# A first convolution in three bf16 products per tap instead of one f32 product

## The chip, the cores and the metric

The kernel runs on one NeuronCore of a Trainium2 chip. The metric is the device time of one execution in microseconds. The engines are named as in the profile: PE is the matrix engine (PEld its weight loads), DVE the vector engine, ACT the scalar engine, POOL GpSimd, and SP the engine from whose queue the transfers are issued. The core has an on-chip memory of 128 partitions (SBUF) and a smaller one into which PE accumulates (PSUM).

## The reference

Four layers follow one another on a tensor x of 64 images, 128 channels, 28x28 points, all f32. Only the first is touched:

```
out = conv3x3(x, quant_weight(w1))          # 128 -> 128 channels, 3x3, padding 1
out = batchnorm(out, gamma1, beta1)         # mean and variance over all images
out = quant_act(out)                        # clip to 0..1, 16 levels
out = conv3x3(out, quant_weight(w2 * m))
out = batchnorm(out, gamma2, beta2) + identity
out = quant_act(out)
```

The quantised weights are odd whole numbers from -15 to 15, divided by 15; the kernel keeps the whole numbers and moves the factor into the batch-norm. The next layers are a self-attention over the points of each image, a Mamba block that scans each image in four directions, and a second Mamba block over eight tokens in each point, with a group-norm and a residual.

## The kernel before, in words

The channels lie on the 128 partitions; an image is 784 columns (T), half an image 392 (HT). The function conv_block does the whole first layer. It begins with the helper quantised, once for each set of weights: a transfer, a Tanh on ACT, the maximum over the row (DVE) and over the partitions (POOL), and a few DVE instructions up to the whole numbers. The last of these, line 168, writes the tile q in the type that the caller names: f32 for the first convolution (line 171), bf16 for the second (line 172).

The first loop (line 175) takes two images at a time, 32 groups in all. A group is loaded into the tile xt (line 177, SP's queue). For each image, conv3x3 makes 18 matmuls: two halves of 14 rows, nine taps each, accumulated in one PSUM bank a half. A tap is a shifted window of the image, cut off at the border, so a matmul has 351 to 392 columns. ACT copies both halves from PSUM to the tile raw (line 182), DVE takes two statistics of it (line 184), and the group is stored to memory (line 185). The batch-norm (line 101 and what follows) needs the statistics of all images. The second loop (line 192) loads the groups again, scales and rounds them (ACT line 196, DVE lines 197 and 199) into the bf16 tile qa, convolves them with the same conv3x3, and copies out and stores image by image (lines 204 to 207). A second batch-norm closes the layer.

The tiles xt, raw, act and qa lie in a pool with three buffers for each name (line 144); the second loop's loads use the name xt too. The PSUM tile acc, one image in two banks, has four buffers. In conv_block the order of instructions on each engine is not written out by hand: the framework orders the traced instructions by the timeline of its own simulation (line 1495), earlier ones first where they can start, and places the waits. Each engine then works in that order.

The attention and the first Mamba block, by contrast, are ordered by a planner in the kernel (class Plan), with costs of its own, and issued in exactly that order (line 469). The token block after them is again left to the framework.

Of the kernel before, what the change touches and what calls it, by code (L numbers as in the profile page):

```python
# [16 lines left out]
F32 = mybir.dt.float32  # L17
BF16 = mybir.dt.bfloat16
AF = mybir.ActivationFunctionType
ALU = mybir.AluOpType  # L20
# [5 lines left out]
C = 128  # L26
HW = 28
T = HW * HW
# [34 lines left out]
def halves(ap):  # L63
    return ap.rearrange("p (h x) -> p h x", h=2)


@with_exitstack
def tile_kernel(ctx: ExitStack, tc: tile.TileContext, x, w1t, w2t, m2t, vecs, pk3, pk4, out):
    nc = tc.nc
    NB = x.shape[0]  # L70

    cpool = ctx.enter_context(tc.tile_pool(name="cpool", bufs=1))
    dram = ctx.enter_context(tc.tile_pool(name="dram", bufs=1, space=DRAM))

    vec = cpool.tile([C, NVEC], F32, name="vec")
    nc.sync.dma_start(vec, vecs)

    def v(name, i=0, p=C):
        a = VEC_AT[name][0] + i
        return vec[:p, a : a + 1]  # L80

    ident = cpool.tile([C, C], F32, name="ident")
    make_identity(nc, ident)
    eps = cpool.tile([C, 1], F32, name="eps")
    nc.vector.memset(eps, BN_EPS)
    x2d = [dram.tile([C, T], F32, name=f"x2d{b}") for b in range(NB)]

    utd = [dram.tile([C, 2, T], F32, name=f"utd{b}") for b in range(NB)]
    ztd = [dram.tile([C, 2, T], F32, name=f"ztd{b}") for b in range(NB)]

    c2d, s2, b2x15 = conv_block(tc, cpool, dram, x, w1t, w2t, m2t, v, eps)
    tables = Tables(tc)
    tables.use(EXP_LN)
    attention_and_mamba(tc, tables, x, c2d, s2, b2x15, x2d, utd, ztd, pk3, pk4, vec, v, ident, eps)
    token_mamba(tc, tables, x2d, utd, ztd, pk4, v, ident, eps, out, NB)


def bn_affine(nc, pool, stats, gamma, beta, unit, eps, name):

    mv = pool.tile([C, 2], F32, name=f"mv{name}")  # L100
    nc.vector.bn_aggr(mv, stats.rearrange("p n s -> p (n s)"))
    std = pool.tile([C, 1], F32, name=f"std{name}")
    nc.scalar.activation(std, mv[:, 1:2], AF.Sqrt, bias=eps, scale=unit * unit)
    rstd = pool.tile([C, 1], F32, name=f"rstd{name}")
    nc.vector.reciprocal(rstd, std)
    s = pool.tile([C, 1], F32, name=f"s{name}")
    nc.vector.tensor_scalar(s, rstd, gamma, unit, ALU.mult, ALU.mult)
    ms = pool.tile([C, 1], F32, name=f"ms{name}")
    nc.vector.tensor_mul(ms, mv[:, 0:1], s)
    b15 = pool.tile([C, 1], F32, name=f"b15{name}")  # L110
    nc.vector.tensor_sub(b15, beta, ms)
    nc.vector.tensor_scalar(b15, b15, 15.0, None, ALU.mult)
    return s, b15


def conv3x3(nc, ps, w, src):

    img = src.rearrange("p (h w) -> p h w", w=HW)
    taps = [(0, 0)] + [(dy, dx) for dy in (-1, 0, 1) for dx in (-1, 0, 1) if (dy, dx) != (0, 0)]
    for half in range(2):  # L120
        acc = ps[:, half, :HT].rearrange("p (h w) -> p h w", w=HW)
        r0 = half * 14
        for i, (dy, dx) in enumerate(taps):
            lo, hi = max(r0, -dy), min(r0 + 14, HW - dy)
            a, b = max(0, -dx), min(HW, HW - dx)
            nc.tensor.matmul(  # L126
                acc[:, lo - r0 : hi - r0, a:b],
                lhsT=w[:, (dy + 1) * 3 + dx + 1, :],
                rhs=img[:, lo + dy : hi + dy, a + dx : b + dx],
                start=(i == 0),  # L130
                stop=(i == len(taps) - 1),
            )


def conv_block(tc, cpool, dram, x, w1t, w2t, m2t, v, eps):
    nc = tc.nc
    NB = x.shape[0]
    GRP = 2
    c1d = [dram.tile([C, GRP, T], F32, name=f"c1d{b}") for b in range(NB // GRP)]
    c2d = [dram.tile([C, T], F32, name=f"c2d{b}") for b in range(NB)]  # L140

    with ExitStack() as ctx:
        wp = ctx.enter_context(tc.tile_pool(name="wq", bufs=1))
        big = ctx.enter_context(tc.tile_pool(name="cv", bufs=3))
        ps = ctx.enter_context(tc.tile_pool(name="cvps", bufs=4, space=PSUM))

        def quantised(name, src, mask, dtype):

            w = wp.tile([C, 9 * C], F32, name="w", tag="wtmp", bufs=2)
            nc.sync.dma_start(w, src)  # L150
            if mask is not None:
                m = wp.tile([C, 9 * C], F32, name="m", tag="wtmp2")
                nc.sync.dma_start(m, mask)
                nc.vector.scalar_tensor_tensor(w, m, 0.5, w, ALU.is_gt, ALU.mult)
            t = wp.tile([C, 9 * C], F32, name="t", tag="wtmp3", bufs=2)
            nc.scalar.activation(t, w, AF.Tanh)
            mx = wp.tile([C, 1], F32, name=f"mx{name}")
            nc.vector.tensor_reduce(mx, t, AX.X, ALU.max, apply_absolute_value=True)
            mxa = wp.tile([C, 1], F32, name=f"mxa{name}")
            nc.gpsimd.partition_all_reduce(mxa, mx, C, bass_isa.ReduceOp.max)  # L160
            r = wp.tile([C, 1], F32, name=f"r{name}")
            nc.vector.tensor_scalar(r, mxa, 2.0, None, ALU.mult)
            nc.vector.reciprocal(r, r)
            nc.vector.tensor_scalar(t, t, r, 0.5, ALU.mult, ALU.add)
            nc.vector.tensor_scalar(t, t, 15.0, MAGIC, ALU.mult, ALU.add)
            nc.vector.tensor_scalar(t, t, MAGIC, 2.0, ALU.subtract, ALU.mult)
            q = wp.tile([C, 9, C], dtype, name=f"q{name}")
            nc.vector.tensor_scalar(q.rearrange("p k c -> p (k c)"), t, 15.0, None, ALU.subtract)  # L168
            return q

        q1 = quantised("1", w1t, None, F32)
        q2 = quantised("2", w2t, m2t, BF16)

        st1 = wp.tile([C, NB * 2, 6], F32, name="st1")
        for g in range(NB // GRP):
            xt = big.tile([C, GRP, T], F32, name="xt")
            nc.sync.dma_start(xt, x[g * GRP : (g + 1) * GRP].rearrange("b c t -> c b t"))
            raw = big.tile([C, GRP, T], F32, name="raw")
            for k in range(GRP):
                acc = ps.tile([C, 2, 512], F32, name="acc")  # L180
                conv3x3(nc, acc, q1, xt[:, k, :])
                nc.scalar.copy(halves(raw[:, k, :]), acc[:, :, :HT])
                for h in range(2):
                    nc.vector.bn_stats(st1[:, (g * GRP + k) * 2 + h, :], raw[:, k, h * HT : (h + 1) * HT])
            nc.sync.dma_start(c1d[g], raw)

        s1, b1x15 = bn_affine(nc, wp, st1, v("gamma1"), v("beta1"), 1.0 / 15.0, eps, "1")
        s1x15 = wp.tile([C, 1], F32, name="s1x15")
        nc.vector.tensor_scalar(s1x15, s1, 15.0, None, ALU.mult)

        st2 = wp.tile([C, NB * 2, 6], F32, name="st2")
        for g in range(NB // GRP):
            ld = big.tile([C, GRP, T], F32, name="xt")
            nc.sync.dma_start(ld, c1d[g])
            act = big.tile([C, GRP, T], F32, name="act")
            nc.scalar.activation(act, ld, AF.Relu, bias=b1x15, scale=s1x15)
            nc.vector.tensor_scalar(act, act, 15.0, MAGIC, ALU.min, ALU.add)
            qa = big.tile([C, GRP, T], BF16, name="qa")
            nc.vector.tensor_scalar(qa, act, MAGIC, None, ALU.subtract)
            for k in range(GRP):  # L200
                acc = ps.tile([C, 2, 512], F32, name="acc")
                conv3x3(nc, acc, q2, qa[:, k, :])
                raw = big.tile([C, T], F32, name="raw2")
                nc.scalar.copy(halves(raw), acc[:, :, :HT])
                for h in range(2):
                    nc.vector.bn_stats(st2[:, (g * GRP + k) * 2 + h, :], raw[:, h * HT : (h + 1) * HT])
                nc.sync.dma_start(c2d[g * GRP + k], raw)

        s2, b2x15 = bn_affine(nc, cpool, st2, v("gamma2"), v("beta2"), 1.0 / 225.0, eps, "2")
    return c2d, s2, b2x15  # L210
# [1288 lines left out]
```

## Time and profile before

| | us |
|---|---|
| median of 3 runs | 14449.58 (14403.58 to 14459.57) |
| profiled execution | 14456.75 |
| its span, first to last instruction | 14454.9 |
| first convolution on PE | 18.6 to 744.6 |
| second convolution on PE | 755.3 to 943.8 |
| PE busy over the span | 10855.2 (75%) |
| DVE busy over the span | 12706.4 (88%) |
| ACT busy over the span | 10460.3 (72%) |
| POOL busy over the span | 11391.7 (79%) |

The span is that of one execution taken by the profiler. The line number in a row (L126) is the line of the kernel that issued the instruction; L126 is the matmul in conv3x3 and serves both convolutions. In a row of the view by time, the first number is the start, the second the duration, both in us, then engine, line, operation, tiles (written <- read), shapes and type, and in brackets how long the engine was idle before and what released it. In a row of the groups, the numbers after the first bar are busy us and the mean ns of one record, those after the second the idle time before. A matmul's record is longer than its share of the stream, because the records of neighbours overlap.

### The profile page before, as it was taken

To read this page: it belongs to the slowest core of one execution; us is meant where nothing else is said; L and a number is where in the kernel's file an instruction comes from. 1 tells how busy PE (TensorE), PEld (TensorE's weight loads), DVE (VectorE), ACT (ScalarE), POOL (GpSimd) and SP (SyncE) were. 2 spreads that over 40 slices of the span, in tenths; PEclk is the share of its full clock that TensorE was granted. 3 is DMA by queue.
4 is the path that set the end of the run, shared out by engine and by line. 5 is a ranking of instruction groups with operands and counts; after the bars stand their busy time and mean duration, and the time that the engine had idled before them with its cause. 6 is when DMAs were issued, how large, how long until landed. Compare 5 with 4: busy or idle time off the path is not lost. (4 is left out here: it accounts for less than half of the span.)

```text
span 14454.9 us, 181149 instructions
## 1 busy us (share of the span) xinstructions
PE 10855.2 (75%) x58370; PEld 7180.2 (50%) x58370; DVE 12706.4 (88%) x13524; ACT 10460.3 (72%) x25236; POOL 11391.7 (79%) x5304
## 2 busy tenths in 40 slices
PE   9987777777777777777776676776767767677676
PEld 5654444444444444444443455555555555555554
DVE  1048999999999999999999799999999999999998
ACT  0047777777777777777777677777777777777776
POOL 0007899889898888889889788888888887888887
PEclk9988888888888888888887787888878888888787
DMA  2243444444444444444444211111112111111111
GB/s 74 72 162 109 135 123 128 129 121 127 131 121 126 130 120 124 133 122 124 134 121 125 67 45 46 55 48 52 45 48 60 44 49 47 49 59 42 49 50 44
DMA packets 711515, 1297.64 MB, mean 90 GB/s; under 512 B 206624, under 2 KB 357536, under 8 KB 710560
## 3 DMA queue, kind: packets, MB, share of 16 engines
q1 hardware_dynamic: 710560, 1286.05, 29.8%
q8 instruction: 460, 7.54, 0.2%
q14 instruction: 495, 4.06, 0.1%
HBM read 954.72 MB, written 330.76 MB: 89 GB/s over the span
## 5 line engine op out<-in xcount | busy, mean ns | idle before, releaser
L228 ACT ACTIVATE a<-delta,A 128x98 f32<-128x98 f32 x14336 | 3906.2, 365 | 1123.2 <-PE y L1317 827.4
L472 POOL TENSOR_TENSOR h<-ur,Br 128x784 f32<-128x784 f32 x1920 | 4205.3, 2216 | 152.6 <-PE y L472 136.3
L1293 POOL TENSOR_TENSOR db<-u,BC 128x896 f32<-128x896 f32 x1568 | 3274.0, 2101 | 856.0 <-DVE h L1312 688.1
L1317 PE MATMUL y<-a,ident 128*128 128x280 f32 x7168 | 2089.5, 455 | 954.2 <-DVE a L1310 898.5
L472 DVE TENSOR_TENSOR_SCAN ah<-ah,h 128x392 f32<-128x392 f32 x2304 | 2303.1, 1000 | 60.8 <-ACT ah L472 50.3
L1317 PEld LDWEIGHTS y<-a,ident 128*128 128x128 f32 x7168 | 1557.7, 221 | 1512.4 <-POOL db L1293 729.1
L472 DVE TENSOR_TENSOR_SCAN h<-a,h 128x784 f32<-128x784 f32 x768 | 1915.0, 2498 | 112.7 <-ACT a L472 57.9
L472 ACT ACTIVATE ah<-dr,A 128x392 f32<-128x392 f32 x2304 | 1322.9, 587 | 612.8 <-DVE ah L472 592.4
L472 POOL TENSOR_TENSOR h<-h,Cr 128x784 f32<-128x784 f32 x640 | 1350.7, 2114 | 357.9 <-DVE h L472 347.5
L1308 DVE TENSOR_TENSOR h<-h,a 128x896 f32<-128x896 f32 x1344 | 1473.7, 1096 | 33.1
L472 DVE TENSOR_TENSOR h<-ah,Cr 128x392 f32<-128x392 f32 x2304 | 1302.5, 565 | 72.9
L472 PE MATMUL y<-h,fold 128*32 128x98 f32 (+1 forms) x12288 | 1024.0, 422 | 385.2 <-DVE h L472 357.2
L1312 DVE TENSOR_TENSOR h<-h,db 128x896 f32<-128x896 f32 x1120 | 1228.2, 1097 | 59.1 <-POOL db L1293 0.5
L472 POOL TENSOR_TENSOR xn<-s,sq 128x784 f32<-128x784 f32 x64 | 136.5, 2133 | 1183.6 <-ACT sq L472 1142.9
L472 PEld LDWEIGHTS bank<-vt,et 112*112 112x112 f32 x6272 | 905.4, 215 | 233.9 <-ACT et L472 90.6
L1310 DVE TENSOR_TENSOR a<-h,BC 128x896 f32<-128x896 f32 x896 | 974.1, 1087 | 21.4
L472 PE MATMUL bank<-vt,et 112*112 112x128 f32 x6272 | 981.6, 320 | 5.0 <-ACT et L472 2.3
L1319 PE MATMUL y<-late,ident 128*128 128x112 f32 x7168 | 848.0, 275 | 14.3 <-DVE late L1310 13.4
L1319 PEld LDWEIGHTS y<-late,ident 128*128 128x128 f32 x7168 | 838.5, 193 | 37.8 <-DVE late L1310 18.0
L472 PEld LDWEIGHTS y<-h,fold 128*32 128x32 f32 x12288 | 378.8, 121 | 909.7 <-DVE h L472 428.8
L472 ACT ACTIVATE a<-dr,A 128x784 f32<-128x784 f32 x768 | 716.8, 942 | 152.0 <-DVE h L472 150.4
L126 PE MATMUL acc<-xt,q 128*128 128x378 f32 (+3 forms) x2304 | 726.0, 478 | 18.6 <-DVE q L168 18.6
(213 smaller groups left out, 20969.2 us busy)
## 6 DMA issues: line engine op xcount, KB each, us to landing
Br<-bcd SPq DMA_DIRECT2D x1536, 98.0 KB, 2.4
Cr<-bcd SPq DMA_DIRECT2D x1536, 98.0 KB, 2.4
dr<-dud SPq DMA_DIRECT2D x1280, 98.0 KB, 2.4
ur<-dud SPq DMA_DIRECT2D x1280, 98.0 KB, 2.3
utd<-tok SPq DMA_DIRECT2D x128, 392.0 KB, 2.7
ztd<-tok SPq DMA_DIRECT2D x128, 392.0 KB, 3.7
rows<-utd SPq DMA_DIRECT2D x192, 256.0 KB, 2.8
xt<-in_x SPq DMA_DIRECT2D x32, 784.0 KB, 5.2
```

The source lines that it names most:

```text
L126: nc.tensor.matmul(acc[:, lo - r0 : hi - r0, a:b], lhsT=w[:, (dy + 1) * 3 + dx + 1, :], rhs=img[:, lo + dy : hi + dy, a + dx : b + dx], st ...
L228: ins = self.tc.nc.scalar.activation(*args, **kw)
L472: last = getattr(getattr(nc, engine), method)(*args, **kw)
L1293: nc.gpsimd.tensor_tensor(x, of_dg(du[:, t, ds, :]), BC[:, t, :NS, :].unsqueeze(1).broadcast_to([C, DB, NS, G]), ALU.mult)
L1308: nc.vector.tensor_tensor(h, h, flat(at(t)), ALU.mult)
L1310: nc.vector.tensor_tensor(by_d(dst), h_d, Cc(t), ALU.mult)
L1312: nc.vector.tensor_tensor(h, h, flat(inject(t)), ALU.add)
L1317: nc.tensor.matmul(y3[:, 1:6], lhsT=ident, rhs=a[:, 0:5, :, n, :], start=False, stop=False)
L1319: nc.tensor.matmul(y3[:, 6:8], lhsT=ident, rhs=late[:, :, :, n, :], start=False, stop=(n == NS - 1))
```

## The change

The weights of both convolutions are now bf16, which holds the whole numbers exactly. The input x is split in SBUF into three bf16 tiles whose sum is x: the first is x rounded to bf16, the second the rounded remainder, the third what then remains. ACT makes the two roundings, DVE the two subtractions; the first subtraction writes over xt. Each tap of the first convolution becomes three bf16 matmuls with the same weights and the same PSUM region, one per part. The second convolution gets a list of one part and so the same matmuls as before. The three new names in the pool have three buffers each, of half the size of an f32 tile.

```
-def conv3x3(nc, ps, w, src):
+def conv3x3(nc, ps, w, parts):
-    img = src.rearrange("p (h w) -> p h w", w=HW)
+    imgs = [m.rearrange("p (h w) -> p h w", w=HW) for m in parts]
...
-            nc.tensor.matmul(
-                acc[:, lo - r0 : hi - r0, a:b],
-                lhsT=w[:, (dy + 1) * 3 + dx + 1, :],
-                rhs=img[:, lo + dy : hi + dy, a + dx : b + dx],
-                start=(i == 0),
-                stop=(i == len(taps) - 1),
-            )
+            for img in imgs:
+                nc.tensor.matmul(
+                    acc[:, lo - r0 : hi - r0, a:b],
+                    lhsT=w[:, (dy + 1) * 3 + dx + 1, :],
+                    rhs=img[:, lo + dy : hi + dy, a + dx : b + dx],
+                    start=(i == 0 and img is imgs[0]),
+                    stop=(i == len(taps) - 1 and img is imgs[-1]),
+                )
...
-            q = wp.tile([C, 9, C], dtype, name=f"q{name}")
+            q = wp.tile([C, 9, C], BF16, name=f"q{name}")
...
             nc.sync.dma_start(xt, x[g * GRP : (g + 1) * GRP].rearrange("b c t -> c b t"))
+            parts = [big.tile([C, GRP, T], BF16, name=f"part{i}") for i in range(3)]
+            nc.scalar.copy(parts[0], xt)
+            nc.vector.tensor_tensor(xt, xt, parts[0], ALU.subtract)
+            nc.scalar.copy(parts[1], xt)
+            nc.vector.tensor_tensor(parts[2], xt, parts[1], ALU.subtract)
             raw = big.tile([C, GRP, T], F32, name="raw")
             for k in range(GRP):
                 acc = ps.tile([C, 2, 512], F32, name="acc")
-                conv3x3(nc, acc, q1, xt[:, k, :])
+                conv3x3(nc, acc, q1, [m[:, k, :] for m in parts])
...
-                conv3x3(nc, acc, q2, qa[:, k, :])
+                conv3x3(nc, acc, q2, [qa[:, k, :]])
```

More of the change, by code (lines that the diff above doesn't have):

```diff
@@ L145, in conv_block, with quantised @@
         ps = ctx.enter_context(tc.tile_pool(name="cvps", bufs=4, space=PSUM))
-        def quantised(name, src, mask, dtype):
+        def quantised(name, src, mask):
             w = wp.tile([C, 9 * C], F32, name="w", tag="wtmp", bufs=2)
@@ L166, in quantised @@
             nc.vector.tensor_scalar(t, t, MAGIC, 2.0, ALU.subtract, ALU.mult)
-            q = wp.tile([C, 9, C], dtype, name=f"q{name}")
+            q = wp.tile([C, 9, C], BF16, name=f"q{name}")
             nc.vector.tensor_scalar(q.rearrange("p k c -> p (k c)"), t, 15.0, None, ALU.subtract)
             return q
-        q1 = quantised("1", w1t, None, F32)
-        q2 = quantised("2", w2t, m2t, BF16)
+        q1 = quantised("1", w1t, None)
+        q2 = quantised("2", w2t, m2t)
         st1 = wp.tile([C, NB * 2, 6], F32, name="st1")
```

## The prediction

> **What bounds the kernel now.** I read the page's 40 slices first, then the kernel before cut into stretches of time, then the instructions of the first convolution in order of time, and last the seams at its two ends. The last digits on the page belong to later stages (VectorE is 88% busy over the whole span), so the change has to be costed in its own stage. Two stretches, the inside of the first and of the second convolution (columns: stretch and its length, then busy us and number of records of PE, PEld, DVE, ACT, POOL, then the granted clock, DMA share, GB/s):
>
> ```profile
> 20.00:740.00 720.00, 720.00 (x2289) 435.75 (x2288) 67.07 (x129) 51.18 (x63) 0.00 (x0) 1.00 0.22 70
> 760.00:940.00 180.00, 180.00 (x1111) 108.18 (x1110) 117.34 (x182) 96.81 (x90) 0.00 (x0) 1.00 0.76 258
> ```
>
> In both, PE never rests, at full clock; the others have much room. The rates differ: the same tap shapes pass as f32 in the first and as bf16 in the second. The groups say how (records, mean ns):
>
> ```profile
> L126 PE MATMUL acc<-xt,q 128*128 128x378 f32 x1024 | 367.3, 481 | 0.0
> L126 PE MATMUL acc<-qa,q 128*128 128x378 bf16 x512 | 127.3, 330 | 0.0
> ```
>
> There are 64 images with 18 products each (9 taps, 2 halves), 1152 in all. The f32 convolution leaves 2304 records, two per product; the bf16 one 1152, one per product. Means of overlapped records are not a rate, so I take the rate from the evictions, one per image. First convolution, in order of time:
>
> ```profile
> 112.03 0.81 ACT L182 COPY raw<-acc 128x784 f32<-128x784 f32 x1 [10.44 <-PE acc L126]
> 123.37 0.81 ACT L182 COPY raw<-acc 128x784 f32<-128x784 f32 x1 [10.53 <-PE acc L126]
> 134.62 0.81 ACT L182 COPY raw<-acc 128x784 f32<-128x784 f32 x1 [10.44 <-PE acc L126]
> ```
>
> 134.62 - 112.03 = 22.59 us for a group of two images (36 products): 0.6275 us a product. Second convolution:
>
> ```profile
> 867.88 0.81 ACT L204 COPY raw<-acc 128x784 f32<-128x784 f32 x1 [2.10 <-PE acc L126]
> 868.85 1.69 ACT L196 ACTIVATE act<-xt,b,s1x 128x1568 f32<-128x1568 f32 x1 [0.16 <-DVE qa L199]
> 870.80 0.81 ACT L204 COPY raw<-acc 128x784 f32<-128x784 f32 x1 [0.26 <-PE acc L126]
> 873.72 0.81 ACT L204 COPY raw<-acc 128x784 f32<-128x784 f32 x1 [2.11 <-PE acc L126]
> ```
>
> 873.72 - 867.88 = 5.84 us for 36 products: 0.1622 us each, 0.26 of an f32 product. The ACTIVATE between two evictions prepares a later group: the order on ACT looks ahead.
>
> The end of the stage is a hard seam. PE's last tap ends near 744.6; the batch-norm needs the statistics of all images:
>
> ```profile
> 746.56 3.62 DVE L101 BATCH_NORM_AGGREGATE mv<-st 128x2 f32<-128x768 f32 x1
> 755.34 44.84 PE L126 MATMUL acc<-qa,q 128*128 128x392 bf16 x267 [10.73 <-DVE qa L199]
> ```
>
> Nothing of the second convolution's arithmetic runs before it, and the attention waits in the same way for the second batch-norm (945.7). So each microsecond taken from PE in this stage comes off the end.
>
> [...] The mean tap has 6724/18 = 373.6 columns (the borders are clipped)[...]; the trace has 162, and I use the trace. [...] the clock here is 1.00 in both stretches. [...] The trace's tensor_tensor of 640 columns (line 543) took 0.827 us[...], so I take 1.80.
>
> **The change part by part.**
> 1. *PE.* Removed: 1152 f32 products x 0.6275 = 722.9 us. Added: 3456 bf16 products of the same columns x 0.1622 = 560.5 us. Difference -162.4 us. The weight loads triple in count to 3456 bf16 ones, mean 98 ns (95 to 152), each beneath a product of 162 ns as in the second convolution; without that cover they would cost 3456 x 0.098 = 339 us. Bounds of the unseen (three products in a row into one region, the same weights loaded three times):[...] at worst nothing that I can price from a row, so 0.170, +27 us.
> 2. *ACT.* Two copies of 1568 columns a group, nearest row the line-196 ACTIVATE, 1.69 us: 3.4 us. With two evictions of 0.81, ACT works 5.0 us in a group of 17.5. Hidden beneath PE.
> 3. *DVE.* Two subtractions, 3.6 us a group, with four statistics of 0.56: 5.8 of 17.5 us. Hidden; POOL is idle here (0.00)[...].
> 4. *The chain.* Copy, subtract, copy, subtract: 1.69+1.80+1.69+1.80 = 7.0 us from landing to third part. It is hidden if it is queued a group ahead: the parts have three buffers, the sums in PSUM four images. A wait enters here: the first part's write waits until PE has released the group three before; behind it on ACT stand evictions, behind the subtractions on DVE the statistics. Both have about two groups (35 us) before PE lacks a PSUM buffer.
> 5. *DMA.* The same transfers. Each group moves 1.6 MB in 17.5 instead of 22.6 us, 92 GB/s; the second convolution moves 258. The input buffer is released after the split, not after PE, so the SP queue's loads start no later. Nothing.
> 6. *The start.* PE starts at 18.57 us, released by the quantised weights. The first input was in by 10.2 us (PE's own wait for it ended there). ACT idles from 6.25 to 13.84, DVE until 12.35 and then works without a gap to 21.8 on the weights. Best case, the split fits around this: 0. Worst, both subtractions stand behind 21.8: 21.8+1.8+1.7+1.8 = 27.1, 8.5 us late. I take +5.
> 7. *The weights* become bf16 in the same line-168 instruction (0.75 us f32, 0.76 bf16 in this trace). Nothing. PE's cold beginning stays: 726.0 - 32 x 22.59 = 3 us before, 188.5 - 32 x 5.84 = 1.6 in the second convolution; -1.
>
> Sum: -162.4 + 5 - 1 = -158. The profiled execution has 14456.75 (span 14454.9, so 1.85 around it): 14298. The median of the runs, 14449.58, is 7.2 below the profiled one: **14291 us**, 1.1% faster. PE's first convolution should end at about 586 instead of 744.6.
>
> **The rivals.**
> - *No look-ahead, slower.* If the split of a group stands behind the evictions of the group before on ACT, PE waits each time 0.81 + 7.0 = 7.8 us, and restarts cold (1.6 us, as at 755): 9.4 x 31 = 291, end 14291+291 = 14582. It decides from 162.4/31 = 5.2 us a group. Against it: the second convolution has the same form (ACT, then two on DVE, three buffers), and PE has no wait inside it, with a group of only 5.84 us. Chance 0.05.
> - *The clock falls.* The bf16 stream lasts 560 us, not 188[...]. For it: later stages stand at 0.8 to 0.86. Against it: those stages leave PE idle at times, while both dense stretches hold 1.00. Chance 0.04.
> - *A later stage moves.* The token stage (from about 7,900 us) is ordered by a simulated timeline that now begins earlier, and its engines could meet differently. The runs' spread, 56 us, is all the profile offers; I let it go to 70 either way around the sum: 14220 to 14360. Against it: its instructions are the same. Chance 0.08.
> - *The stream is slower, but steady*, 0.17 to 0.21 a product, so that the gain melts (0.2092 is break-even): about 14380. Against it: weight loads have 64 ns to spare. Chance 0.03.
>
> **How the numbers follow.** The likeliest case has 0.80: 14255 to 14325 (start 0 to 8.5,[...] and the spread of medians). A measurement of this kernel tells about 0.5%, 72 us, from no change. Faster by more than that needs less than 14377: the likeliest, nearly all of the moved stage, a little of the rest, 0.88; same 0.06; slower 0.06. The range for 8 in 10 takes in the moved stage's bounds in part: 14235 to 14350.
>
> **What the profile will show.** Right: 3456 bf16 records in the first convolution, evictions 8.76 us apart, clock 1.00, PE idle about 11 us at the seam near 590, and every later stage the same length but about 158 us sooner. Wrong: PE waits on the parts in each group (rival one), a spacing above 0.17 us, a clock below 1.00, or a mamba or token stage that changes its length.

## The result and the profile after

The changed kernel takes 14291.59 us (median of 4 runs, 14284.76 to 14303.03) against 14450.95 for the kernel before (4 runs, 14403.58 to 14459.57): a ratio of 0.9897, 95% interval 0.9875 to 0.9919. The forecast was 14291, faster by 1.1%. The profiled execution took 14284.76, its span is 14283.0.

In the changed kernel line 127 is the matmul, lines 181 and 183 are the copies of the split, 182 and 184 its subtractions, and 189 copies the sums out of PSUM. The two convolutions, cut as before (busy us and records of PE, PEld, DVE, ACT, POOL, then clock, DMA share, GB/s):

```profile
30.00:580.00 550.00, 550.00 (x3392) 330.81 (x3391) 166.63 (x184) 135.17 (x121) 0.00 (x0) 1.00 0.25 90
610.00:780.00 170.00, 170.00 (x1050) 102.20 (x1049) 110.45 (x173) 89.79 (x84) 0.00 (x0) 1.00 0.75 254
```

PE is as full as before (550.00 us of 550), at a clock of 1.00, and now passes through the first convolution at the pace of the second: 162 ns a record in both (550/3392 and 170/1050). DVE is busy 166.63 us of the 550 where it had 67.07 of 720, ACT 135.17 where it had 51.18; both are idle for more than half of the stretch. The groups of the first convolution, with what is new on ACT and DVE:

```profile
L127 PE MATMUL acc<-part,q 128*128 128x378 bf16 x1536 | 297.0, 329 | 0.0
L182 DVE TENSOR_TENSOR xt<-xt,part 128x1568 f32<-128x1568 f32 x32 | 57.3, 1791 | 233.1 <-ACT part L181 233.1
L184 DVE TENSOR_TENSOR part<-xt,part 128x1568 bf16<-128x1568 f32 x32 | 57.3, 1793 | 18.0 <-ACT part L183 18.0
L183 ACT CAST part<-xt 128x1568 bf16<-128x1568 f32 x32 | 48.0, 1499 | 34.4 <-DVE xt L182 34.4
L181 ACT CAST part<-xt 128x1568 bf16<-128x1568 f32 x32 | 47.7, 1497 | 219.7 <-PE acc L127 219.7
```

Read the idle time on the right. The first copy (L181) waits 219.7 us in all for PE, because its buffer is still being read; the first subtraction waits for that copy. These are waits of engines that are ahead of PE. In order of time, inside the stage of the changed kernel:

```profile
304.15 1.50 ACT L181 CAST part<-xt 128x1568 bf16<-128x1568 f32 x1 [7.59 <-PE acc L127]
305.56 0.81 ACT L189 COPY raw<-acc 128x784 f32<-128x784 f32 x1
305.68 1.79 DVE L182 TENSOR_TENSOR xt<-xt,part 128x1568 f32<-128x1568 f32 x1 [8.05 <-ACT part L181]
307.51 1.50 ACT L183 CAST part<-xt 128x1568 bf16<-128x1568 f32 x1 [1.15 <-DVE xt L182]
309.04 1.79 DVE L184 TENSOR_TENSOR part<-xt,part 128x1568 bf16<-128x1568 f32 x1 [0.62 <-ACT part L183]
313.26 0.81 ACT L189 COPY raw<-acc 128x784 f32<-128x784 f32 x1 [4.26 <-PE acc L127]
323.08 0.80 ACT L189 COPY raw<-acc 128x784 f32<-128x784 f32 x1
```

From 305.56 to 323.08 a group takes 17.52 us, three times the 5.84 of the second convolution and where the f32 kernel took 22.59. The chain copy, subtract, copy, subtract runs from 304.15 to 310.83, 6.7 us. The buffer that PE released at about 304 us is one of three, so PE comes to the new part two groups of 17.52 us later, some 28 us after the split is done (an estimate from these rows). The evictions are not evenly spaced, 7.70 and 9.82 us: the one at 305.56 stands behind the copy on ACT. PE does not notice: it is busy for 550.00 us of the 550 from 30 to 580.

PE waits for the parts at the start only. The waits of PE in the first convolution (us in total, times, longest), and its first pieces in order of time:

```profile
PE acc L127 <- DVE q L169: 17.9, 1, 17.9
PE acc L127 <- DVE part L184: 1.8, 1, 1.8
PE acc L127 <- ACT part L183: 1.1, 1, 1.1
```

```profile
17.95 2.14 PE L127 MATMUL acc<-part,q 128*128 128x392 bf16 x6 [17.95 <-DVE q L169]
21.18 0.81 PE L127 MATMUL acc<-part,q 128*128 128x392 bf16 x2 [1.09 <-ACT part L183]
23.84 16.39 PE L127 MATMUL acc<-part,q 128*128 128x392 bf16 x91 [1.85 <-DVE part L184]
```

The seam between the convolutions is what it was, 10.73 us of idle PE, 160 us sooner:

```profile
586.69 3.62 DVE L101 BATCH_NORM_AGGREGATE mv<-st 128x2 f32<-128x768 f32 x1
595.47 9.79 PE L127 MATMUL acc<-qa,q 128*128 128x392 bf16 x45 [10.73 <-DVE qa L206]
```

Cutting both profiled executions at the same events gives, in us:

| stage | before | after |
|---|---|---|
| start to PE's first product | 18.6 | 17.9 |
| first convolution, to its last eviction | 726.0 | 566.9 |
| seam and second convolution, to its last eviction | 199.2 | 200.1 |
| opening of the attention, to the first sum of the scans | 203.9 | 187.5 |
| attention and Mamba scans | 6917.7 | 6920.5 |
| from there to the token block's first sum | 110.8 | 109.9 |
| token block's sums | 6230.8 | 6232.2 |
| rest | 47.9 | 48.0 |

159.1 us of the gain lie in the first convolution. The spans differ by more, 171.9; 16.4 of that lie in the opening of the attention, which the change does not touch.

### The profile page after: what moved, and what is told of

It reads as the page before. It is cut to its first block, busy times and chain, and to the rows that moved or that the text cites. A ratio compares the mean times of both kernels' runs of the same rounds, so it can differ in the third digit from the quotient of the medians.

```text
span 14283.0 us, 183617 instructions
## 1 busy us (share of the span) xinstructions
PE 10677.9 (75%) x59522; PEld 7055.9 (49%) x59522; DVE 12818.7 (90%) x13588; ACT 10550.2 (74%) x25300; POOL 11389.1 (80%) x5304
## 5 line engine op out<-in xcount | busy, mean ns | idle before, releaser
L479 PE MATMUL wide<-kt,qt 16*112 16x392 f32 x1792 | 500.4, 597 | 223.6 <-ACT e L479 216.7
```

The lines of the kernel that those rows point to most:

```text
L479: last = getattr(getattr(nc, engine), method)(*args, **kw)
```

## The experiments

The theory was: PE's stream alone sets this stage, each 16-bit product costs 0.1622 us whatever else is done, and the split costs nothing because it is made ahead. Rivals: a floor set by preparation or transfers; a split that only seems free; a rate that depends on three products in a row with the same weights. The runs with two parts, with one buffer, with the idle split and with fp16 were measured beside the kernel before, whose median there was 14437.82 us (15 runs); their ratios are to that.

**Two parts.**

```
-            parts = [... for i in range(3)]
+            parts = [... for i in range(2)]
...
-            nc.vector.tensor_tensor(parts[2], xt, parts[1], ALU.subtract)
```

> The third part of x is left out, so each tap has two bf16 products and the convolution sees x to 16 bits of mantissa; one subtraction a group is left out with it. Theory (PE's stream alone sets the length of the stage, 0.1622 us a product): 1152 products fewer, -186.9 us against the changed kernel's 14291.6, so 14105 us, evictions 5.84 us apart and the first convolution 567 - 187 = 380 us long. Rival (part of the stage is fixed by the preparation on ACT and DVE or by the transfers): clearly less than -187, evictions further apart than 5.84 us, PE with waits inside the stage.

14102.52 us, ratio 0.9773 (0.9758 to 0.9789). The first convolution takes 376.1 us, 190.8 less than with three parts; 1152 x 0.1622 is 186.9, and 2.9 are the waits at the start, which are gone. The last 1.0 is not explained. PE runs the stage without a gap:

```profile
19.63 376.04 PE L127 MATMUL acc<-part,q 128*128 128x392 bf16 x2304 [19.63 <-DVE q L169]
```

**One part.** The same edit, down to a single part: one copy and no subtraction. It convolves x rounded to bf16, so it is a measure of the stage and not a kernel to use.

> The second and third parts are left out, so the convolution sees x rounded to bf16; one product a tap, one copy a group, no subtraction. Theory (PE's stream alone): evictions 2.92 us apart, first convolution 1152 x 0.1622 = 187 plus about 2 for the cold start, 189 us, some 13910 us in all. Rival (at 5.84 us a group another engine or the transfers, 1.6 MB a group or 275 GB/s, take over): evictions further apart than 2.92 us and PE with waits inside the stage.

13889.03 us in one execution, 21 less than expected; the token block's sums are shorter in it (6193.1 us, against 6232.2 in the changed kernel's profile), which this edit does not touch. The first convolution takes 189.6 us, and evictions are 5.84 us apart for two images:

```profile
30.00:200.00 170.00, 170.00 (x1050) 102.20 (x1048) 60.72 (x118) 86.25 (x86) 0.00 (x0) 1.00 0.77 274
```

PE is still full, with 274 GB/s moved. So 189.6, 376.1 and 566.9 us for one, two and three parts lie nearly on one line, 186.5 us for the second part and 190.8 for the third, waits included: no floor is in sight even where the stage is a third as long.

**One buffer for each part.**

```
-            parts = [big.tile([C, GRP, T], BF16, name=f"part{i}") for i in range(3)]
+            parts = [big.tile([C, GRP, T], BF16, name=f"part{i}", bufs=1) for i in range(3)]
```

> The changed kernel with one buffer for each part in place of three, so that a group cannot be split before PE has used up the group before. Theory (the split is hidden only because it is made ahead): PE waits for the chain in each of 31 groups, 7.2 us for the chain alone to 9.4 us with a cold restart, +223 to +291 us, so 14515 to 14583 us, slower than the kernel before (14451). Rival (the split costs PE little even without being ahead, since the first products need only the first part): under +50 us, below 14340.

14529.28 us, ratio 1.0067 (1.005 to 1.0084): slower than the kernel before. The first convolution takes 815.2 us, 248.3 more than with three buffers, 8.0 in each of 31 groups. One of them in order of time:

```profile
90.93 1.50 ACT L181 CAST part<-xt 128x1568 bf16<-128x1568 f32 x1 [7.35 <-PE acc L127]
92.46 1.79 DVE L182 TENSOR_TENSOR xt<-xt,part 128x1568 f32<-128x1568 f32 x1 [7.81 <-ACT part L181]
92.48 0.49 PE L127 MATMUL acc<-part,q 128*128 128x392 bf16 x2 [1.32 <-ACT part L181]
94.29 1.50 ACT L183 CAST part<-xt 128x1568 bf16<-128x1568 f32 x1 [1.15 <-DVE xt L182]
95.82 1.79 DVE L184 TENSOR_TENSOR part<-xt,part 128x1568 bf16<-128x1568 f32 x1 [0.62 <-ACT part L183]
95.84 0.81 PE L127 MATMUL acc<-part,q 128*128 128x392 bf16 x2 [2.87 <-ACT part L183]
97.66 18.53 PE L127 MATMUL acc<-part,q 128*128 128x392 bf16 x104 [1.01 <-DVE part L184]
```

PE waits for each link of the chain in turn, 1.32, 2.87 and 1.01 us. The group of records with 392 columns, to which the first products of every half image belong, sums these waits over the stage:

```profile
L127 PE MATMUL acc<-part,q 128*128 128x392 bf16 x768 | 190.0, 343 | 184.8 <-ACT part L183 88.8 <-ACT part L181 40.9 <-DVE part L184 37.3
```

Without the 17.8 us before PE's first product these are 167 us, where the changed kernel has 2.9: 164 of the 248. The rest, 84, is slower running: over the inside of this stage the clock's mean is 0.87, not 1.00. In the group shown it is 0.59 up to 100.67 us and 0.99 to 1.00 after it, so what is lost lies at the restart.

```profile
20.00:830.00 810.00, 643.62 (x3435) 358.70 (x3435) 176.12 (x192) 140.93 (x125) 0.00 (x0) 0.87 0.18 63
92.48:100.67 8.19, 4.31 (x14) 1.91 (x14) 4.51 (x4) 2.16 (x2) 0.00 (x0) 0.59 0.48 159
100.67:107.00 6.33, 6.33 (x40) 3.77 (x39) 0.00 (x0) 0.00 (x0) 0.00 (x0) 0.99 0.13 51
107.00:116.00 9.00, 9.00 (x57) 5.45 (x56) 1.04 (x2) 0.84 (x2) 0.00 (x0) 1.00 0.00 0
```

So the gain hangs on the buffers: the same arithmetic with no look-ahead loses all of it and 92 us more.

**The split beside f32 products.** The kernel before, with the two copies and two subtractions added into tiles that nothing reads; a tile rest takes the remainder, since xt is still needed.

```
+            parts = [... for i in range(3)]
+            rest = big.tile([C, GRP, T], F32, name="rest")
+            nc.scalar.copy(parts[0], xt)
+            nc.vector.tensor_tensor(rest, xt, parts[0], ALU.subtract)
+            nc.scalar.copy(parts[1], rest)
+            nc.vector.tensor_tensor(parts[2], rest, parts[1], ALU.subtract)
```

> The kernel before with its f32 products, and in addition the split of each group into three bf16 parts (two copies on ACT, two subtractions on DVE, into tiles that nothing reads). Theory (the split is hidden beneath PE): the kernel before plus 0 to 9 us, 14451 to 14460, evictions 11.3 us apart. Rival (the split disturbs PE or the order of the work): more than 9 us, at most the whole split in line, 32 x 7.0 = 224 us, 14675.

14433.15 us against 14437.82, ratio 0.9999 (0.9991 to 1.0008). The 14451 to 14460 expected stood on the first comparison's median, 13 us above this one. The first convolution takes 724.7 us, against 725.2 to 726.1 in four profiles of the kernel before. DVE and ACT do more than twice their work in the same 720 us, and PE is as full as before:

```profile
20.00:740.00 720.00, 720.00 (x2292) 435.84 (x2291) 179.68 (x194) 141.04 (x123) 0.00 (x0) 1.00 0.22 70
```

**All taps of a part, then the next part.**

```
-        for i, (dy, dx) in enumerate(taps):
...
-            for img in imgs:
+        for j, img in enumerate(imgs):
+            for i, (dy, dx) in enumerate(taps):
...
```

> The changed kernel with the two inner loops of conv3x3 exchanged: all nine taps of the first part, then of the second, then of the third, so that each product has other weights than the one before. Theory (each product loads its weights again anyway, hidden beneath the stream): the first convolution stays at 561 to 567 us and evictions at 8.76 us. PE could start up to 3 us better, since the first part alone feeds nine products. Rival (the rate of 0.1622 us leans on three products in a row with the same weights): evictions more than 1% further apart, over 8.85 us.

The first convolution takes 562.9 us. Two evictions of equal place in their groups:

```profile
301.48 0.81 ACT L189 COPY raw<-acc 128x784 f32<-128x784 f32 x1 [1.42 <-PE acc L127]
319.00 0.81 ACT L189 COPY raw<-acc 128x784 f32<-128x784 f32 x1 [1.42 <-PE acc L127]
```

17.52 us again, with other weights for every product: the rate does not lean on repeated weights. PE runs all 3456 products in one piece: of the 4.0 us less, 2.9 are the waits at the start, which are gone. The single execution, 14270.75, is too little to tell a gain of 4 us in the total.

**Two fp16 parts.** The slope of 187 us a part says that fewer parts are the way on. Two parts of fp16, 11 bits of mantissa each, keep far more of x than two of bf16; the second part rounds the remainder, so the split is no longer exact.

```
+F16 = mybir.dt.float16
...
+        q1 = quantised("1", w1t, None, F16)
...
-            parts = [big.tile([C, GRP, T], BF16, name=f"part{i}") for i in range(3)]
+            parts = [big.tile([C, GRP, T], F16, name=f"part{i}") for i in range(2)]
             nc.scalar.copy(parts[0], xt)
-            nc.vector.tensor_tensor(xt, xt, parts[0], ALU.subtract)
-            nc.scalar.copy(parts[1], xt)
-            nc.vector.tensor_tensor(parts[2], xt, parts[1], ALU.subtract)
+            nc.vector.tensor_tensor(parts[1], xt, parts[0], ALU.subtract)
```

> x split into two fp16 parts (11 bits each), weights of the first convolution in fp16, so two products a tap, one rounding and one subtraction a group. Theory (number of 16-bit products, whatever the type): 14105 us, as with two bf16 parts, evictions 5.84 us apart. Rival (fp16 runs at another rate than bf16 or its weight loads are not hidden): evictions further apart; at the f32 spacing of 0.3138 us a record it would be about 14450.

14077.4 us, ratio 0.9754 (0.9739 to 0.9768): faster than both kernels, and 28 us below what was expected. The first convolution takes 376.8 us, as with two bf16 parts:

```profile
19.80 376.71 PE L128 MATMUL acc<-part,q 128*128 128x392 f16 x2304 [19.80 <-DVE q L170]
```

That accounts for 190 us against the changed kernel; the two medians, taken apart from one another, differ by 214. The rest is not in this stage, and I don't claim it for fp16: the token block's sums took 6208.9 us in this profile, 6232.2 and 6243.4 in two of the changed kernel's, and 6210.3 to 6232.7 in four of the kernel before.

**The opening of the attention.** The 16 us that were in no step of the sum asked for more profiles, of the two kernels unchanged.

> The kernel before, unchanged, profiled once more, to see its later stages. In its first profile the opening of the attention (last eviction of the second convolution to the first sum of the Mamba scan) took 203.9 us, with PE's clock at 0.50 for 40 us of it; in the changed kernel 187.5. Theory (that difference is chance, the clock of one execution, not the change): 187 to 192 us this time, and a span nearer to 14440. Rival (the f32 convolution leaves the opening slower): 200 to 205 us again.

214.6 us: long again, so chance as a cause was in doubt. But the kernel with f32 products and the idle split had 187.8, and the one with one bf16 part 204.1, so it wasn't the f32 convolution.

> The kernel before, unchanged, profiled a third time. Its opening of the attention took 203.9 and 214.6 us in two profiles; kernels with the split took 187 to 191 in six. Theory (chance of one execution[...]): some profiles of the kernel before show 187 to 192 us. Rival (the kernel before is bound to the slow opening): 203 us or more again.

> The kernel before, unchanged, profiled a fourth time; as for the third: 187 to 192 us by chance, or 203 us and more by the rival.

> The changed kernel, unchanged, profiled a second time. Theory (chance): the opening of the attention may be 187 to 192 us or over 203. The first convolution is 567 us again, and the total follows the sum of its stages.

188.3 and 187.8 us for the kernel before, 187.7 for the changed one, whose first convolution took 567.2 us this time. The rival falls: the same kernel shows 188 and over 203. What differs is PE's clock, seen in the same stretch of two executions of the kernel before. The first profile:

```profile
944.00:984.00 40.00, 15.69 (x60) 9.19 (x60) 18.76 (x62) 7.14 (x10) 0.00 (x0) 0.52 0.32 103
984.00:1024.00 40.00, 36.95 (x152) 27.89 (x151) 8.22 (x17) 12.75 (x29) 0.00 (x0) 0.50 0.00 1
```

The third:

```profile
944.00:984.00 40.00, 16.08 (x62) 9.54 (x63) 18.99 (x63) 6.89 (x10) 0.00 (x0) 0.54 0.31 103
984.00:1024.00 40.00, 31.41 (x195) 23.19 (x194) 10.89 (x23) 22.53 (x40) 0.00 (x0) 0.88 0.13 41
```

Both open at about half clock. In the first, the next 40 us stay at 0.50 although PE is busy for 36.95 of them; in the third the clock is 0.88, and 195 records pass in place of 152. That is in step with the longer opening, though no run changes the clock alone. Why the clock rises in one execution and not in the other these runs don't show.

## Why the prediction was right

The total was forecast as 14291 and measured as 14291.59. That is closer than the method can claim, since the runs of the changed kernel alone spread over 18 us; the stage is the better test, and there most steps hold to a few us.

- *PE's stream.* Forecast -162.4 us from 3456 x 0.1622. Measured: 17.52 us a group, exactly three times 5.84; -159.1 for the stage with its beginning. The lower end of the likeliest case, 14255, stood in part on a faster rate than this, an estimate of the author's that no run shows. The rate taken from the same shapes in the other convolution carried over to other data, other weights in sequence and a third type.
- *Weight loads.* Covered: 98 ns each beneath 162, and none shows in the stage's length, whether the weights repeat (566.9 us) or not (562.9).
- *ACT.* The copies take 1.50 us, not the 1.69 of the nearest row. That row also reads a scale and a bias (s1x, b), the copy neither; no run here takes these operands away one by one, so what the 0.19 us between the two rows consist of is not shown. It changed nothing, since the step is hidden.
- *DVE.* 1.79 us (1791 and 1793 ns in the two groups) against 1.80. The 1.80 was the author's estimate: the one row that it names, 827 ns for 640 columns, does not give it alone. A line through that row and the 1096 ns for 896 columns of another of the kernel before (L1308) does, an estimate from two rows; a third with 896 columns (L1305) took 2059 in the mean, from 1073 up.
- *The chain.* Forecast 7.0 us and hidden; 6.7 measured, and PE waits nowhere for it after the start. The run with one buffer shows that the look-ahead is the reason. It prices the rival too: 8.0 us a group against a forecast of 7.2 to 9.4, and a time of 14529 where the rival's text had 14582. The rival's chain was too long, since PE takes up each part as it comes (5.2 us of waits in the group shown, not 7.8), and its restarts too cheap (84/31 = 2.7 us a group, not 1.6).
- *The start.* I took +5 out of 0 to 8.5. PE began 0.6 us sooner than before and then lost 2.9 in two waits; the first convolution ended at 584.8, forecast 586. The -1 for PE's slow beginning did not come: 566.9 - 32 x 17.52 leaves 6.3 us, 3.4 without the waits, where the kernel before had 3 and the sum took 1.6. What was seen of such beginnings is fewer records: in the kernel before, 7 in the 4 us from 18.60 and 14 in the 4 us from 26.60, with the clock at 1.00 in both; in its second convolution, 17 in the 4 us from 755.34, at 0.66, and 27 in the next 4 us, at 1.00.
- *Clock, later stages.* The clock is 1.00 in the stage, from 30 to 580 us. The later stages keep their lengths within some 27 us in executions of one and the same kernel (in the kernel before the opening of the attention by 27, the token block's sums by 22). The profiled pair differs by 171.9 us, and the 13 beyond the stage are of that size. The medians differ by 159.4, nearly the stage's 159.1, but that is chance too: the interval of the ratio allows 117 to 181 us; against the 14437.82 of the later 15 runs the changed kernel's median is 146 us lower, and on one more chip the kernel before took 14430.09 to 14437.72 in three executions and the changed kernel 14295.58 in one, 135 to 142 less. What holds is the stage: 725.2 to 726.1 us in four profiles before, 566.9 and 567.2 in two after.

So the gain in the stage was not luck, but that the total fell within 1 us was: the median of 3 runs from which the forecast subtracted lies 12 us above that of the later 15.

## What to carry to other kernels

Where PE fills a stage with f32 products and one operand is exact in 16 bits, count the records: one f32 product here cost 3.87 of 16-bit ones (0.6275 us against 0.1622), so a split in three gains over a fifth of the stage and a split in two, which no longer keeps all of x, nearly half. The split is free only while it runs ahead: count its chain against the buffers, since with one buffer the same change cost 0.7%. And take the gain from the stage between two hard seams, not from two totals, whose other stages wander by as much as 27 us.

## What the runs showed of the hardware

fp16 passed at the rate of bf16 (376.8 and 376.1 us for 2304 products). PE's clock can stay at 0.50 for 40 us in which PE is busy for 37, after 40 us in which it was busy for 16, in some executions of an unchanged kernel and not in others (3 of the 12 profiles here); in those the opening of the attention took 203.9 to 214.6 us instead of 187.5 to 191.0.
